# Moving the transposes and stores of aggregates into a later gather: a two-layer graph network on one NeuronCore

## The chip, the cores and the metric

The kernel runs on one core of a Trainium2 chip. The metric is device time in microseconds, from one launch. Of the kernel before there are three runs, and one further execution was recorded by the hardware profiler. A core has five engines that run side by side, each working through its own queue of instructions in the order in which it was laid down: TensorE (PE in the profile; its weight loads are PEld), VectorE (DVE), ScalarE (ACT), GpSimd (POOL) and SyncE (SP, which issues DMAs here). They wait for each other through semaphores.

## What is computed

There are 16 graphs of 1024 nodes with 64 channels, an adjacency matrix for each, and a node mask. The first layer takes, for every node and channel, weighted quantiles over the values of the node's neighbours that are left after some edges have been removed by rank. A small two-layer network follows. The second layer is three graph convolutions. Cut to its core:

```python
h = relu(layernorm(x))
neigh = (adj_ > 0) & ~eye                 # neighbours, without the node itself
rank = cumsum(neigh) - neigh              # a neighbour's number in its row
skip = max(where(nb > 10, (nb + 1) // 2, 1), 1)
rem = neigh & (skip > 1) & (rank % skip == skip - 1) & mask
nd = where(rem | rem.T, 0, adj_) > 0      # live neighbours and the node itself
s = sort(where(nd[..., None], h[:, None], inf), axis=2)
for tau, w in ((0.25, 0.25), (0.5, 0.5), (0.75, 0.25)):
    pos = tau * (nv - 1)                  # nv: live entries of the node
    agg += w * (s[floor(pos)] + frac(pos) * (s[ceil(pos)] - s[floor(pos)]))
x = x + (relu((h + agg) @ W1 + b1) @ W2 + b2) * mask
h = relu(layernorm(x))
x1 = bn(relu(adj @ (h @ W1) + b1)); x2, x3 in the same way from x1, x2
out = x + relu(concat(x1, x2, x3) @ Wl + bl)
```

## The kernel before

**Pairs and blocks.** The graphs are worked on in eight pairs. The 64 channels of the two graphs of a pair fill the 128 partitions. The nodes of a graph are put in the order of their number of live neighbours, `place` holding each node's place. The 1024 places are cut into seven blocks (`BLOCKS`: 0 to 200, 200 to 392, 392 to 592, 592 to 768, 768 to 888, 888 to 960, 960 to 1008) and a tail of 16 (`TAIL`, 1008 to 1024). A block has a fixed number of slots for each node's neighbours, from 11 in the first to 42 in the tail, so that a sort of fixed shape fits all of its nodes.

**Preparing a pair (`prepare`, lines 651 to 842).** Layer norm, the edges and their transpose, the removal of edges (lines 722 to 742, with the result `edge` by ScalarE on line 744 and the sort key on line 750), the rows in their new order through DRAM, and a number for every live neighbour, `r`. This is written as a generator. It is run eleven steps at a time, between the blocks of the pair before, so that both are in flight together.

**A block (`gather_block`, `sort_block`).** `gather` (line 936) goes through the slots in chunks of `per`, about 400 columns together. For each slot VectorE compares `r` with the slot's number, which gives a one-hot tile `s` (line 962; there are two buffers). TensorE multiplies it with the node features, in three bf16 parts, into `pg` (line 993; three buffers in PSUM). ScalarE copies `pg` into the block's `g` (line 998; two buffers of whole blocks). A sort on VectorE follows, a fixed list of minima and maxima over slots (line 920), then the quantiles' coefficients (line 925) and their sum (line 933) into `agg`, one tile of 128 x 1024 per pair.

**Storing.** As soon as 128 further columns of `agg` are complete, `store` (line 1000) has TensorE transpose them (line 1005, into `pt_agg`, one buffer), ScalarE copy the result into `o` (line 1007, two buffers), and ScalarE issue one DMA for each graph of the pair (line 1009) into `agg_d` in DRAM. A pair gives eight such transposes: block 0 gives one, block 1 two, block 2 one, block 3 two, block 4 none, blocks 5 and 6 one each. Pairs 0 to 6 do not sort their tails at once. They lay them down in `tail_d`, and `sort_tails` sorts those of pairs 0 to 3 during pair 4 and those of pairs 4 to 6 during pair 7, with a transpose for each pair; pair 7 sorts its own. That makes 72 transposes in all.

**The order of the work.** The loop of lines 1367 to 1384 has one step per block n: eleven steps of the next pair's preparation, the gather of block n + 1, then the sort of block n, at the end of which its stores are issued. The last pair runs with `later` instead (lines 1389 to 1406), the second half of the network for all pairs, seven steps per block, and what is left of it at the end. `later` reads `agg_d` by an indirect DMA (line 1172). `done.sent` tells how many pairs have been stored completely when the program is built, and an assertion in `first` compares with it. The order in the program is a priority, not yet the order of a queue: a planner lays down each engine's queue ahead of the run, with durations of its own, always taking the ready instruction that stands first in the program. On the chip each queue is then followed as it stands.

The functions that the change touches:

Of the kernel before, what the change touches and what calls it, by code (L numbers as in the profile page):

```python
# [41 lines left out]
TAIL = (1008, 1024, 21, 42)  # L42
# [317 lines left out]
def missing_high(slots, least):  # L360

    return range(slots - 1, least, -2)
# [37 lines left out]
def graph_layers_kernel(ctx: ExitStack, tc: tile.TileContext, ins, out: bass.AP):  # L400
    nc = tc.nc
# [5 lines left out]
    NP = NB // 2  # L407
# [6 lines left out]
    ident = const.tile([P, P], F32, name="ident")  # L414
# [129 lines left out]
    def bias(value):  # L544

        if value not in biases:
            t = const.tile([P, 1], F32, name=f"bias{len(biases)}")
            nc.vector.memset(t, value)
            biases[value] = t
        return biases[value]  # L550
# [22 lines left out]
    TW = TAIL[1] - TAIL[0]  # L573
# [362 lines left out]
    def gather(st, block, g, pools):  # L936


        work, ps, _ = pools
        j0, j1, least, slots = block  # L940
        first, end, fewer = NEAR[(BLOCKS + (TAIL,)).index(block)]
        W = j1 - j0
        high = missing_high(slots, least)
        r, at = (st.r[0], j0) if j1 <= SPLIT else (st.r[1], j0 - SPLIT)
        per = max(1, min(HALF // W, 400 // W))
        for k0 in range(0, slots, per):
            n = min(per, slots - k0)

            w0 = fewer.get(k0, 0)
            if w0 == W:  # L950
                w0 = 0
            chunks = [
                range(
                    max([c for c in first if k0 + k >= first[c]], default=0),
                    min([c for c in end if k0 + k < end[c]], default=NT),
                )
                for k in range(n)
            ]
            s = work.tile([P, n, 2, NT, W], BF16, tag="s", bufs=2, name="s")
            for k, us in enumerate(chunks):  # L960
                us = slice(us.start, us.stop)
                nc.vector.tensor_scalar(  # L962
                    s[:, k, :, us, w0:], r[:, :, us, at + w0 : at + W], float(LIVE + 1 + k0 + k), None, ALU.is_equal
                )
            pg = ps.tile([P, n, W], F32, tag="pg", bufs=3, name="pg")
            looks = [(u, [k for k in range(n) if u in chunks[k]]) for u in range(NT)]
            looks = sorted((look for look in looks if look[1]), key=lambda look: -len(look[1]))
            whole = len(looks[0][1]) == n and not w0
            if not whole:
                for x in range(2):  # L970

                    nc.tensor.matmul(
                        out=pg[x * C : (x + 1) * C].rearrange("p k w -> p (k w)"), lhsT=ident_h[C:, :C],
                        rhs=st.hp[C:].rearrange("p a x t c -> p (a x t c)")[:, : n * W], start=True, stop=False,
                    )
            for i, (u, ks) in enumerate(looks):
                if i == whole:
                    for k in range(n):
                        if k0 + k + 1 not in high:
                            continue  # L980
                        none = work.tile([P, W], BF16, tag="none", bufs=2, name="none")
                        nc.scalar.activation(
                            none, st.nvs[:, j0:j1], AF.Relu, bias=bias(k0 + k + 0.5), scale=-1.0
                        )
                        for x in range(2):
                            half = slice(x * C, (x + 1) * C)
                            nc.tensor.matmul(
                                out=pg[half, k], lhsT=ident_big[:, half], rhs=none, start=False, stop=False
                            )
                ks = slice(ks[0], ks[-1] + 1)  # L990
                for part in range(3):
                    for x in range(2):
                        nc.tensor.matmul(  # L993
                            out=pg[x * C : (x + 1) * C, ks, w0:], lhsT=st.hp[:, part, x, u, :],
                            rhs=s[:, ks, x, u, w0:], start=(whole and i == 0 and part == 0),
                            stop=(i == len(looks) - 1 and part == 2),
                        )
            nc.scalar.copy(g[:, k0 : k0 + n, :], pg)  # L998

    def store(p, agg, cols, place0, pools):  # L1000

        work, ps, _ = pools
        n = cols.stop - cols.start
        pt = ps.tile([P, P], F32, tag="small", bufs=1, name="pt_agg")
        nc.tensor.transpose(pt[:n, :], agg[:, cols], ident)
        o = work.tile([P, P], F32, tag="o", bufs=2, name="o")
        nc.scalar.copy(o[:n, :], pt[:n, :])
        for x in range(2):
            nc.scalar.dma_start(out=agg_d[2 * p + x][place0 : place0 + n, :], in_=o[:n, x * C : (x + 1) * C])

    def gather_block(st, n, pools):
        work, ps, rows = pools
        block = (BLOCKS + (TAIL,))[n]
        j0, j1, _, slots = block
        if n == 0:
            for q in range(len(TAUS)):
                nc.gpsimd.tensor_copy(tail_z[:, q, st.p, :], st.z[:, q, TAIL[0] : TAIL[1]])
        st.g[n] = rows.tile([P, slots, j1 - j0], F32, tag="g", bufs=2, name="g")
        gather(st, block, st.g[n], pools)

    def sort_block(st, n, pools):

        work, ps, rows = pools
        if n == len(BLOCKS) and st.p < NP - 1:
            nc.scalar.dma_start(out=tail_d[st.p][:, :, :], in_=st.g[n])
            return
        block = (BLOCKS + (TAIL,))[n]
        j0, j1, _, slots = block
        if n == 0:
            st.agg = work.tile([P, N], F32, tag="agg", bufs=1, name="agg")  # L1030
            st.done = 0
        t = rows.tile([P, plan(block)[3], j1 - j0], F32, tag="t", bufs=1, name="t")
        quantiles(work, block, (st.g[n], t), st.z[:, :, j0:j1], st.agg[:, j0:j1])
        while st.done + P <= j1 or (j1 >= TAIL[0] and st.done < j1):
            cols = slice(st.done, min(st.done + P, j1))
            store(st.p, st.agg, cols, st.done, pools)
            st.done = cols.stop

    def sort_tails(first, end, pools):

        work, ps, rows = pools
        W = (end - first) * TW
        g = rows.tile([P, TAIL[3], W], F32, tag="g", bufs=2, name="g_tails")
        for p in range(first, end):
            nc.scalar.dma_start(out=g[:, :, (p - first) * TW : (p - first + 1) * TW], in_=tail_d[p][:, :, :])
        t = rows.tile([P, plan(TAIL)[3], W], F32, tag="t", bufs=1, name="t_tails")
        agg = work.tile([P, W], F32, tag="agg_tails", name="agg_tails")
        quantiles(work, TAIL, (g, t), tail_z[:, :, first:end].rearrange("p q p2 w -> p q (p2 w)"), agg)
        for p in range(first, end):
            store(p, agg, slice((p - first) * TW, (p - first + 1) * TW), TAIL[0], pools)  # L1050


    def channels_first(pools, src, tag):
# [295 lines left out]
    with ExitStack() as stack:  # L1349
        keep = stack.enter_context(tc.tile_pool(name="keep", bufs=1))  # L1350
        pools = (
            stack.enter_context(tc.tile_pool(name="work", bufs=1)),
            stack.enter_context(tc.tile_pool(name="ps", bufs=1, space=PSUM)),
            stack.enter_context(tc.tile_pool(name="rows", bufs=1)),
        )
        last = len(BLOCKS)
        with ExitStack() as inner:
# [7 lines left out]
            st = ahead.result  # L1365
            gather_block(st, 0, pools)
            for p in range(NP - 1):
# [16 lines left out]
                st = ahead.result  # L1384


        with ExitStack() as inner:
            one = inner.enter_context(tc.tile_pool(name="late", bufs=1))
            late = (one, inner.enter_context(tc.tile_pool(name="ps_late", bufs=2, space=PSUM)))
            done = Pair()  # L1390
            done.sent = TAILS[NP - 1][0]
            ahead = Steps(later(late, done))
            for n in range(last + 1):
                for _ in range(STEPS):
                    ahead.step()
                if n == 0:
                    sort_block(st, n, pools)
                    gather_block(st, n + 1, pools)
                    sort_tails(*TAILS[NP - 1], pools)
                    done.sent = NP - 1  # L1400
                    continue
                if n < last:
                    gather_block(st, n + 1, pools)
                sort_block(st, n, pools)
            done.sent = NP
            ahead.rest()

# [45 lines left out]
```

## Time and profile before

| | us |
|---|---|
| three runs: median (lowest, highest) | 3244.12 (3240.37, 3251.95) |
| the profiled execution's own time | 3232.01 |
| its span, first instruction to last | 3230.2 |
| TensorE busy, with 27819 matmuls | 2602.9 (81%) |
| VectorE busy | 2569.1 (80%) |
| ScalarE busy | 1714.2 (53%) |
| one transpose on line 1005 (median of the 65 from `agg`) | 0.328 |
| one copy on line 1007 (median of 72) | 0.266 |
| one DMA issue on line 1009 (median of 144) | 0.345 |
| the first transpose of aggregates, the last | 279.9, 2913.8 |

The profile has one row for each group of instructions: the line in the kernel, the engine, the operation, the tile written and those read, and how many. A timeline row gives the start and the length in microseconds, and in brackets how long the engine had been idle before it and what ended that. A row of the list of waits gives who waited for whom, the total in microseconds, how often, and the longest. The mean granted TensorE clock was 0.902 of full speed.

### The profile page before, as it was taken

The numbers are of one execution on the slowest core, as the hardware profiler recorded it, in microseconds if no ns is written. First come the engines' busy times: TensorE is split into PE (matmuls) and PEld (weight loads), VectorE is DVE, ScalarE is ACT, GpSimd is POOL, SyncE is SP. The second block draws the span as 40 slices with busy tenths as digits, with TensorE's granted clock in tenths as the row PEclk, the third lists the DMA queues.
The fourth block names the chain that finished last, engine by engine and source line by source line (L and its number), as shares of the span: only waits on it lengthen the run. The fifth ranks groups of instructions, "written<-read, shape, count | busy, mean of one in ns | idle before, by whom it ended". The sixth has DMA issues, their size and how long they took to land. (4 is left out here: it accounts for less than half of the span.)

```text
span 3230.2 us, 67236 instructions
## 1 busy us (share of the span) xinstructions
PE 2602.9 (81%) x27819; PEld 1728.7 (54%) x27849; DVE 2569.1 (80%) x5895; ACT 1714.2 (53%) x3292; POOL 461.8 (14%) x545
## 2 busy tenths in 40 slices
PE   3689968987898689867686799689976689898878
PEld 2446645664566357545463466456644356565545
DVE  4149999899889988998997889988996888793332
ACT  4777647655766566666464666476553223242221
POOL 4111020110011001200112010201112120221110
PEclk9779989998999799988797799889988799899999
DMA  4131113011311130114001211130102110222211
GB/s 136 46 105 66 37 44 123 33 35 32 118 33 37 42 107 33 51 54 97 31 17 45 91 48 34 45 117 32 39 21 61 21 42 17 54 55 53 53 53 41
DMA packets 221082, 177.45 MB, mean 55 GB/s; under 512 B 189024, under 2 KB 189152, under 8 KB 216672
## 3 DMA queue, kind: packets, MB, share of 16 engines
q1 hardware_dynamic: 141824, 125.88, 12.7%
q0 software_dynamic: 17408, 37.81, 3.8%
q10 hardware_dynamic: 61536, 9.39, 1.9%
q8 instruction: 219, 3.59, 0.5%
q14 instruction: 95, 0.78, 0.1%
HBM read 124.44 MB, written 48.55 MB: 54 GB/s over the span
## 5 line engine op out<-in xcount | busy, mean ns | idle before, releaser
L993 PE MATMUL pg<-s,hp 128*64 128x400 bf16 (+11 forms) x16848 | 1361.8, 314 | 93.2 <-DVE s L962 92.7
L993 PEld LDWEIGHTS <-hp 128*64 128x64 bf16 x16848 | 907.4, 113 | 452.1 <-issue 75.3
L962 DVE TENSOR_SCALAR s<-r 128x3200 bf16<-128x3200 bf16 (+25 forms) x1312 | 621.1, 520 | 144.2 <-PE pg L993 143.9
L998 ACT COPY g<-pg 128x400 f32<-128x400 f32 (+10 forms) x384 | 168.5, 442 | 478.2 <-PE pg L993 440.4
L920 DVE TENSOR_TENSOR t<-g 128x600 f32<-128x600 f32 (+9 forms) x524 | 319.8, 628 | 12.9 <-ACT g L998 11.1
L770 POOL DMA_INDIRECT live_d<-edge,place x128 | 175.4, 1371 | 1025.3 <-DVE place L765 870.9
L1129 PE MATMUL pg<-adjT,xw 128*64 128x512 fp8e4 x2304 | 285.5, 400 | 39.6 <-DVE xw L1119 28.9
L920 DVE TENSOR_TENSOR g<-t 128x96 f32<-128x96 f32 (+16 forms) x555 | 285.8, 539 | 1.4
L855 ACT ACTIVATE coef<-z,bias 128x200 f32<-128x200 f32 (+6 forms) x480 | 174.8, 402 | 140.9 <-DVE agg L933 133.7
L1129 PEld LDWEIGHTS <-xw 128*64 128x64 bf16 x2304 | 144.7, 115 | 163.1 <-DVE xw L1119 30.3
L1172 POOL DMA_INDIRECT agg<-agg_d,place x128 | 139.4, 1089 | 535.7 <-PE pt L1060 412.8
L920 DVE TENSOR_TENSOR t<-t 128x192 f32<-128x192 f32 (+20 forms) x447 | 208.5, 478 | 0.4
L796 PE MATMUL pt<-ident_h,lp 128*128 128x128 bf16 x1024 | 102.3, 261 | 120.8 <-DMA lp<-live_d 71.1
L786 POOL DMA_DIRECT2D lp<-live_d x128 | 87.5, 685 | 774.0 <-PE pt L796 745.4
L664 DVE SCALAR_TENSOR_TENSOR junk_v<-a 128x1024 fp8e4<-128x1024 f32 x128 | 156.3, 1221 | 49.2 <-DMA a<-in_adj 49.0
L858 ACT ACTIVATE coef<-coef,wcol 128x200 f32<-128x200 f32 (+7 forms) x512 | 190.7, 399 | 3.5 <-issue 2.2
L799 ACT ACTIVATE liveT<-pt 128x1024 fp8e4<-128x1024 f32 x128 | 129.9, 1024 | 98.7 <-PE pt L796 97.6
L838 ACT CAST r<-pr 128x592 bf16<-128x592 f32 (+1 forms) x256 | 143.5, 587 | 48.6 <-PE pr L834 47.4
L832 PE MATMUL pr<-liveT,upto 128*128 128x512 fp8e4 (+2 forms) x384 | 124.7, 343 | 50.3 <-ACT r L838 41.3
L796 PEld LDWEIGHTS <-lp 128*128 128x128 fp8e4 x1024 | 82.9, 117 | 145.0 <-DMA lp<-live_d 101.0
L762 ACT ACTIVATE junk<-keys,minus 128x1024 fp8e4<-128x1024 f32 x128 | 144.4, 1128 | 29.8 <-PE keys L755 28.7
L744 ACT ACTIVATE edge<-q,bias 128x1024 fp8e4<-128x1024 f32 x128 | 142.0, 1110 | 33.1 <-PE q L739 29.1
(182 smaller groups left out, 3956.6 us busy)
## 6 DMA issues: line engine op xcount, KB each, us to landing
a<-in_adj SPq DMA_DIRECT2D x128, 512.0 KB, 3.4
adjT_d<-edgeT SPq DMA_DIRECT2D x16, 1024.0 KB, 4.4
lp<-live_d POOLq DMA_DIRECT2D x128, 128.0 KB, 2.3
adjT<-adjT_d SPq DMA_DIRECT2D x16, 1024.0 KB, 6.3
room<-in_x SPq DMA_DIRECT2D x16, 256.0 KB, 3.2
h_d<-room SPq DMA_DIRECT2D x16, 256.0 KB, 2.9
h_again<-h_d SPq DMA_DIRECT2D x16, 256.0 KB, 3.8
xt<-in_x SPq DMA_DIRECT2D x16, 256.0 KB, 4.7
```

The costliest lines, as they stand in the source:

```text
L664: nc.vector.scalar_tensor_tensor(junk, a, 1.0, a, ALU.is_equal, ALU.not_equal, accum_out=odd[:, b, t : t + 1], saturate=False)
L762: nc.scalar.activation(junk, keys, AF.Sign, bias=minus[:, t : t + 1], accum_out=above[:, t : t + 1], saturate=False)
L770: sent = nc.gpsimd.indirect_dma_start(out=live_d[b][:, :], out_offset=bass.IndirectOffsetOnAxis(ap=place[:, b, t : t + 1], axis=0), in_=ed ...
L796: nc.tensor.matmul(out=pt[:, u, :], lhsT=lp[:, u * P : (u + 1) * P], rhs=ident_h, start=True, stop=True)
L838: nc.scalar.copy(st.r[side][:, x, u, :], pr[:, : j1 - j0])
L855: nc.scalar.activation(coef[:, i, :], z[:, at], AF.Abs, bias=bias(rank - (slots + 1) // 2 + tau), scale=sign)
L858: nc.scalar.activation(coef[:, i, :], coef[:, i, :], AF.Relu, bias=wcol[:, q : q + 1], scale=-w)
L920: nc.vector.tensor_tensor(view(bufs, o, n1, n2), view(bufs, a, n1, n2), view(bufs, b, n1, n2), ALU.max if op else ALU.min)
L962: nc.vector.tensor_scalar(s[:, k, :, us, w0:], r[:, :, us, at + w0 : at + W], float(LIVE + 1 + k0 + k), None, ALU.is_equal)
L993: nc.tensor.matmul(out=pg[x * C : (x + 1) * C, ks, w0:], lhsT=st.hp[:, part, x, u, :], rhs=s[:, ks, x, u, w0:], start=(whole and i == 0 an ...
L998: nc.scalar.copy(g[:, k0 : k0 + n, :], pg)
L1129: nc.tensor.matmul(out=pg[cs, :], lhsT=part[:, u, cs], rhs=adjT[x][:, u, sl], start=(u == 0 and k == 0), stop=(u == NT - 1 and k == len(xw ...
```

## The change

`gather` now remembers the last matmul of its last chunk that starts at or before half of the slots, and returns it. Where `sort_block` and `sort_tails` called `store`, they now put the call's arguments on a list, `waiting`. `gather_block` calls `send` after it has traced its gather: `send` runs `store` for all that waits, and every transpose gets an edge to the remembered matmul. That edge carries no semaphore. It only tells the planner that the transpose comes later in TensorE's queue than that matmul. Since block n is sorted after the gather of block n + 1, its stores come with the gather of block n + 2. They move past all of that gather in the program's order, and so do their copies on ScalarE and the DMA issues on ScalarE's queue. Block 6's go with the first gather of the next pair. In pairs 4 and 7, where block 0 is sorted ahead of the gather of block 1, block 0's go with the gather of block 1, and those of `sort_tails` with the gather of block 2. At the end of the last pair a last `send`, without the edge, stores block 6 and the tail.

```diff
-                        nc.tensor.matmul(
+                        summed = nc.tensor.matmul(
                             out=pg[x * C : (x + 1) * C, ks, w0:], lhsT=st.hp[:, part, x, u, :],
...
             nc.scalar.copy(g[:, k0 : k0 + n, :], pg)
-
-    def store(p, agg, cols, place0, pools):
+            if k0 <= slots // 2:
+                halfway = summed
+        return halfway
+
+    waiting = []
+
+    def send(pools, after=None):
+        for one in waiting:
+            store(*one, pools, after)
+        waiting.clear()
+
+    def store(p, agg, cols, place0, pools, after=None):
...
-        nc.tensor.transpose(pt[:n, :], agg[:, cols], ident)
+        turned = nc.tensor.transpose(pt[:n, :], agg[:, cols], ident)
+        if after is not None:
+            tc.add_manual_dep(
+                turned.ins, after.ins.name,
+                mybir.DependencyInfo(mybir.DependencyClass.NoSync, mybir.DependencyReason.SCHED_ONLY),
+                reason="the aggregates are late",
+            )
...
-        gather(st, block, st.g[n], pools)
+        send(pools, gather(st, block, st.g[n], pools))
...
-            store(st.p, st.agg, cols, st.done, pools)
+            waiting.append((st.p, st.agg, cols, st.done))
...
-            store(p, agg, slice((p - first) * TW, (p - first + 1) * TW), TAIL[0], pools)
+            waiting.append((p, agg, slice((p - first) * TW, (p - first + 1) * TW), TAIL[0]))
...
                     sort_tails(*TAILS[NP - 1], pools)
-                    done.sent = NP - 1
                     continue
                 if n < last:
                     gather_block(st, n + 1, pools)
                 sort_block(st, n, pools)
+                done.sent = NP - 1
+            send(pools)
             done.sent = NP
             ahead.rest()
```

## The prediction

> **What bounds the kernel now.** I first read the busy times: TensorE is busy 2602.9 us (81%), VectorE 2569.1 us (80%), ScalarE 53%. No engine is full, so the two busiest must be waiting for each other. The chain of waits reaches back only to 3088 us, 142 us before the end, a stretch that belongs to the second layer, so it says nothing of the change. The list of waits, longest first in total, does:
>
> ```profile
> PE pt_agg L1005 <- DVE agg L933: 96.3, 23, 11.3
> PE pg L993 <- DVE s L962: 92.7, 40, 12.2
> DVE s L962 <- PE pg L993: 143.9, 69, 21.3
> ```
>
> The first line is what the change aims at: 23 times TensorE stood at the transpose of a block's aggregates until VectorE had written them, 96.3 us together, 3.0% of the span. The second and third say that TensorE otherwise waits for the one-hot tiles `s`, and VectorE for TensorE to free them. A microsecond taken from the first line is a gain only where the second does not take it over and VectorE is itself waiting.
>
> Then I listed the 72 transposes with the idle time ahead of each. Seven of them, one per pair (at 481, 788, 1096, 1407, 1785, 2099 and 2404 us), hold 5 x 10.29 + 11.33 + 9.72 = 72.5 us of the 96.3. TensorE's timeline at the third, then VectorE's:
>
> ```profile
> 1084.85 0.53 PE L993 MATMUL pg<-s,hp 128*64 128x32 bf16 x24
> 1095.66 0.47 PE L1005 MATMUL pt_agg<-ident,agg 128*128 128x128 f32 x1 [10.29 <-DVE agg L933]
> 1097.80 1.21 PE L993 MATMUL pg<-s,hp 128*64 128x400 bf16 x6 [1.67 <-DVE s L962]
> ...
> 1089.55 0.19 DVE L962 TENSOR_SCALAR s<-r 128x160 bf16<-128x160 bf16 x1
> ...
> 1095.38 0.23 DVE L933 TENSOR_TENSOR agg<-coef 128x72 f32<-128x72 f32 x1
> 1095.52 3.84 DVE L962 TENSOR_SCALAR s<-r 128x224 bf16<-128x224 bf16 x34
> ```
>
> Here TensorE has finished block 6's gather (1085.4). Next are the transpose of block 5's aggregates and the gather of the last 16 nodes, whose first chunk needs 25 one-hot instructions. VectorE slips these singly between the sort steps of block 5, and most come after `agg`. TensorE stops again at 1097.80 for that very tile. VectorE is without a gap from 1076 to 1106.
>
> The other 16 waits hold 96.3 - 72.5 = 23.8 us. The largest group, five of 1.85 to 2.35 us, lies where a pair's first block is finished beside the matmuls that remove the next pair's edges (lines 728 to 742). At 1204.98 TensorE waits 2.34 us, and VectorE later goes idle for TensorE:
>
> ```profile
> 1204.98 0.33 PE L1005 MATMUL pt_agg<-ident,agg 128*128 128x128 f32 x1 [2.34 <-DVE agg L933]
> ...
> 1220.78 0.17 DVE L750 SCALAR_TENSOR_TENSOR key<-nv,node 128x8 f32<-128x8 f32 x1 [1.34 <-ACT edge L744]
> 1237.84 1.91 DVE L962 TENSOR_SCALAR s<-r 128x3200 bf16<-128x3200 bf16 x2 [0.70 <-PE pg L993]
> 1241.90 1.58 DVE L962 TENSOR_SCALAR s<-r 128x2800 bf16<-128x2800 bf16 x2 [2.15 <-PE pg L993]
> 1245.96 0.64 DVE L962 TENSOR_SCALAR s<-r 128x1824 bf16<-128x1824 bf16 x1 [2.48 <-PE pg L993]
> ```
>
> From 1221 to 1251 TensorE is the bound, so a lead it brings into this stretch reaches the next sort.
>
> **What the Trainium skill says.** "TensorE: Matmul & The Clock Gate", section on the array and engine queue depths: TensorE may pull weight loads ahead, but its matmuls keep program order; ScalarE and VectorE are strict first in, first out. The trace agrees: no gather matmul passes the transpose in the 10.29 us, and VectorE's one-hots keep their place behind the sort. The same page, section on PE-mode transpose: the result lands in PSUM and has to be copied out. Here that copy is 0.27 us on ScalarE (72 of them). "Perfetto Trace Analysis", section on identifying the most-contended engine: matmul busy share is a poor measure of headroom. That agrees with a TensorE at 81% that gates VectorE in one stretch and waits for it in the next.
>
> **The change, part by part.**
>
> 1. The seven tail waits. Removed: 10.29 us and the transpose itself. In its place TensorE goes straight to line 993, which cannot start before its tile is written, at 1097.80. VectorE's queue there has no gap to move into, so the wait of 1.67 us becomes one of 10.29 + 0.47 + 1.67 = 12.4 us. Gain 0, for all seven (each is followed within 2.14 us by a wait of 1.66 or 1.67 us for `s`). If the one-hots did come earlier, 72.5 us would be free; nothing in the edit touches VectorE's code, so I take 0.
>
> 2. The waits of 1.85 to 3.28 us. I followed each to the next idle time of VectorE that TensorE or its follower ended; the lead is worth the smaller of the two. At 586 and 896 us TensorE next waits 0.5 us for `key` on a VectorE that has no gap: 0. At 1205, 1894 and 2205 us VectorE waited for that removal's result 1.34, 1.11 and 1.28 us: 3.73. At 1658 us: 0.21. At 2338 us VectorE then waits 0.76 and 1.23 us for TensorE: 1.99. At 2623 us the lead runs into VectorE's wait of 10.41 us for a gather DMA: 0. Sum 5.9 us. The small ones (0.2 to 0.84 us, 3.4 us together): I take 1. Together 7 us; bounds 0 and 23.8.
>
> 3. ScalarE and the stores. Per block 0.27 us of copy and two DMA issues (median 0.345 us each) move along, 72 and 144 of them. They now stand between the copies of `g` in mid-gather. With ScalarE 53% busy and three `pg` buffers they are hidden; without that cover they would cost 72 x 0.96 = 69 us. One place can gain: where pair 4 sorts the tails, the stores' issue is held up behind the tails' loads.
>
> ```profile
> 1507.36 8.31 ACTq L1009 DMA_DIRECT2D agg_d<-o  x2
> 1515.72 0.48 ACT L998 COPY g<-pg 128x384 f32<-128x384 f32 x1 [11.50 <-issue]
> ```
>
> Block 0's store now comes lower in priority than the whole gather of block 1, so the copies of `g` may pass it, up to 8.3 us. But TensorE then waits 5.10 and 11.75 us for VectorE (1541.87, 1572.69), and VectorE itself waits for the tails' loads until 1517.81. I take 0, bound 8.
>
> 4. The transposes' new place. 72 x 0.33 us = 24 us of TensorE time exists before and after. Before, the two of block 1 stand at the end of the TensorE-bound stretch (1250.75, 1251.43); now they stand in block 3's gather, where VectorE is sorting. Block 0's goes into that stretch from just ahead of it. I count 0, between -5 (two of 0.33 us in eight pairs) and +10. Where two follow each other, the second needs the one `pt_agg` buffer emptied: at most 0.35 us x 16 pairs of transposes = 6 us, hidden if other matmuls stand between, as now. By the middle of that gather the aggregates are ready: the gather fills a `g` buffer which the same sort has to release first. So the new order adds no wait of its own.
>
> 5. Buffers and the end. `agg` is freed by block 6's transpose, which moves into the next pair's first gather; it stands at 1136.66 now, and `agg` is next written by that pair's first sort, which ends at 1204.92, 68 us later. The last pair's stores (2879.72, 2913.81) go after the last sort; the gather DMAs that read them run at 3090. Both hidden. `done.sent` gates only what the builder may issue.
>
> 6. The static order. The order on every engine is laid down before the run from a planner's times. Moving 72 transposes shifts those times by fractions of a microsecond, and may swap one-hots and sort steps on VectorE. The trace can't show the new order; it bounds the size. Between successive tail transposes equal work of one pair takes 307.1, 307.3, 310.9, 313.3 and 305.3 us (the interval with tails left out), so orders and clocks of this kind differ by up to 4 us from their middle. Over 8 pairs that is -24 to +32 us. I take 0.
>
> Sum: -7 us. The profiled execution took 3232.0 us (span 3230.2, 1.8 around it) and would take 3225. It lies 12.1 us below the median of the runs, 3244.1, so by that measure the forecast is **3237 us**.
>
> **The rivals.** What a measurement of this kernel can tell from no change is about 0.3%, 9.7 us: 3234.4 to 3253.9.
>
> - A, the likeliest: the waits are absorbed as worked out, and the order hardly moves. 3237, own range 3229 to 3250. For it: the 1.67 us behind every 10.29.
> - B, faster: the leads of part 2 pass whole (23.8 us), or the new order suits the pairs by 3 us each. 3244 - 24 = 3220. For it: 143.9 us in which VectorE waits for TensorE. Against: two of eight pairs show the lead absorbed at `key`.
> - C, slower: the planner's VectorE list shifts. In each pair, where a sort ends inside the TensorE-bound gather, a chunk's two one-hots (1.9 us) fall behind one combining step (L925, 1.6 us), and TensorE waits 3.5 us. 8 x 3.5 = 28, less the 7: 3265. It decides from (7 + 9.7) / 8 = 2.1 us per pair. For it: the waits come back at the same spot of every pair, so one bad swap counts eight times. Against: the one-hots' code and priorities are unchanged.
> - D: the tail waits go too, because the one-hots move ahead of the sort: 3244 - 96 = 3148. Against it: the sort of block 5 is issued ahead of that gather in the program.
>
> **How the numbers follow.** A 0.50 (0.13 of it below 3234.4, 0.33 within, 0.04 above), B 0.22, C 0.26, D 0.02. Faster 0.13 + 0.22 + 0.02 = 0.37, same 0.33, slower 0.04 + 0.26 = 0.30. The range 3212 to 3270 holds A, the middle of B and C, and part 6's bounds in most of their length; about 0.1 is left out on each side. The likeliest case's own range is 3229 to 3250.
>
> **What would show it.** Right: the line of waits for `agg` at L1005 is all but gone (under 5 us); the wait of `pg` for `s` grows by some 70 us, with 12 us waits once per pair at the tail gather; VectorE's busy time is within 1%. Part 2: no 2 us wait in the removal's matmuls, `key` 1.3 us earlier in its pair. Wrong: VectorE's order differs between the two kernels by more than single instructions, the pairs' period leaves 305 to 313 us, ScalarE waits at the stores' issue in mid-gather, or the tail waits shrink.

## The result, and the profile after

The changed kernel took 3235.66 us in the median of 20 runs, the kernel before 3244.82 us in 20 runs beside it: ratio 0.9968, 95% interval 0.9956 to 0.9980, 9.2 us less between the medians. Measured twice more with the experiments it came to 0.9930 (0.9906 to 0.9955) and 0.9929 (0.9907 to 0.9950). So it is faster, by some 9 to 23 us. The forecast was 3237 us, by a gain of 7 us. On this occasion the number was met; on the later two the gain was about three times the forecast. The experiments show that the reason given for it was not what made the kernel faster.

The profiled execution of the changed kernel has a span of 3234.3 us. That is above the 3230.2 us of before's profile, which happened to be a short execution, so the two spans say nothing of the gain; the single stretches do. First the list of waits (who waited for whom, total us, how often, longest):

```profile
PE pg L993 <- DVE s L962: 150.6, 31, 15.0
...
DVE s L962 <- PE pg L993: 111.1, 62, 9.1
...
PE pt_agg L1017 <- ACT o L1025: 16.2, 7, 2.6
```

The 96.3 us in which TensorE waited for `agg` at the transposes are gone. In their place its wait for `s` grew by 58 us (92.7 before), and there is a new line: transposes that wait for a copy by ScalarE, 16.2 us, nearly nothing before. VectorE's waits for TensorE fell by 33 us (143.9 before; a second profile of before has 128.2, so not all of that is the change). The timeline at the third tail's gather, the place the prediction began with:

```profile
1097.30 0.53 PE L993 MATMUL pg<-s,hp 128*64 128x32 bf16 x24
...
1107.57 0.23 DVE L933 TENSOR_TENSOR agg<-coef 128x72 f32<-128x72 f32 x1
1107.72 3.85 DVE L962 TENSOR_SCALAR s<-r 128x224 bf16<-128x224 bf16 x34
...
1110.00 1.21 PE L993 MATMUL pg<-s,hp 128*64 128x400 bf16 x6 [12.17 <-DVE s L962]
```

The transpose no longer stands ahead of the tail's gather, and TensorE waits 12.17 us for the one-hots instead. The prediction had said 12.4.

Where, then, did time go? The end of each block's `agg` on VectorE cuts the span into stretches. Of the six stretches from one pair's block 6 to the next, five are 302 to 312 us in both profiles and differ by 0 to 4 us. Pair 4's is 381.2 us before and 359.7 after. In its middle the timeline of the kernel before has this (`live_d` are the scatters by which POOL writes the rows of the next pair's second graph in their new order, `lp` the loads that read them back):

```profile
1684.62 4.10 POOL L770 DMA_INDIRECT live_d<-edge,place  x1 [8.30 <-DVE place L765]
...
1689.02 14.40 POOL L770 DMA_INDIRECT live_d<-edge,place  x1 [0.30 <-issue]
...
1703.73 1.22 POOL L770 DMA_INDIRECT live_d<-edge,place  x1 [0.30 <-issue]
...
1711.01 0.96 POOL L770 DMA_INDIRECT live_d<-edge,place  x1 [0.30 <-issue]
...
1714.41 1.89 PE L796 MATMUL pt<-ident_h,lp 128*128 128x128 bf16 x16 [22.35 <-DMA lp<-live_d]
...
1728.65 1.53 DVE L962 TENSOR_SCALAR s<-r 128x1152 bf16<-128x1152 bf16 x4 [21.31 <-PE pg L993]
```

and the changed kernel, at the same place:

```profile
1689.52 4.54 POOL L770 DMA_INDIRECT live_d<-edge,place  x1 [8.12 <-DVE place L765]
...
1694.37 1.96 POOL L770 DMA_INDIRECT live_d<-edge,place  x1 [0.30 <-issue]
...
1696.63 1.26 POOL L770 DMA_INDIRECT live_d<-edge,place  x1 [0.30 <-issue]
...
1705.00 1.18 POOL L770 DMA_INDIRECT live_d<-edge,place  x1 [0.30 <-issue]
...
1708.63 1.98 PE L796 MATMUL pt<-ident_h,lp 128*128 128x128 bf16 x16 [11.88 <-DMA lp<-live_d]
...
1721.51 1.86 DVE L962 TENSOR_SCALAR s<-r 128x1152 bf16<-128x1152 bf16 x5 [9.10 <-PE pg L993]
```

Before, the second of eight scatters took 14.40 us, where the six behind it take 0.96 to 1.5 (the first takes 4.1 to 4.5 in both kernels). The eight lasted 27.3 us (1684.62 to 1711.97), after the change 16.7 us. TensorE waits for the loads that follow, 22.35 us against 11.88, and VectorE for TensorE, 21.31 us against 9.10. The diff touches none of these lines.

It does touch the planner: of VectorE's 5768 instructions in the program's main part 2070 stand at another place in the queue than before, of ScalarE's 3010 others than the stores 1189, of TensorE's 27106 others 8734, of SyncE's 293 45, of POOL's none. So two things changed at once, the place of the stores and the order of everything else.

### The profile page after: what moved, and what is told of

It is laid out like the page before. It is cut to its first block, busy times and chain, and to the rows that moved or that the text cites. A ratio compares the mean times of both kernels' runs of the same rounds, so it can differ in the third digit from the quotient of the medians.

```text
span 3234.3 us, 67196 instructions
## 1 busy us (share of the span) xinstructions
PE 2614.8 (81%) x27819; PEld 1721.7 (53%) x27849; DVE 2568.1 (79%) x5895; ACT 1710.7 (53%) x3292; POOL 468.4 (14%) x545
## 5 line engine op out<-in xcount | busy, mean ns | idle before, releaser
L993 PE MATMUL pg<-s,hp 128*64 128x400 bf16 (+11 forms) x16848 | 1379.6, 314 | 183.0 <-DVE s L962 150.6
L770 POOL DMA_INDIRECT live_d<-edge,place x128 | 159.1, 1243 | 983.9 <-DVE place L765 835.8
L796 PE MATMUL pt<-ident_h,lp 128*128 128x128 bf16 x1024 | 108.9, 274 | 91.9 <-DMA lp<-live_d 45.3
L662 ACT ACTIVATE edge<-a 128x1024 fp8e4<-128x1024 f32 x128 | 133.8, 1055 | 44.2 <-DMA a<-in_adj 43.7
```

Source lines behind the costliest of these rows:

```text
L770: sent = nc.gpsimd.indirect_dma_start(out=live_d[b][:, :], out_offset=bass.IndirectOffsetOnAxis(ap=place[:, b, t : t + 1], axis=0), in_=ed ...
L993: summed = nc.tensor.matmul(out=pg[x * C : (x + 1) * C, ks, w0:], lhsT=st.hp[:, part, x, u, :], rhs=s[:, ks, x, u, w0:], start=(whole and ...
```

## The experiments

**Order or stores.** Both can be held. The program is traced twice: once to learn the planner's queues, and once with an edge from every instruction to the next in each queue, the stores' own instructions left free. An edge of this kind carries no semaphore.

```diff
     with tile.TileContext(nc) as tc:
         graph_layers_kernel(tc, ins, out, late, stores)
+        for engine, order in like.items():
+            mine = by[engine]          # traced, stores left out
+            for a, b in zip(order, order[1:]):
+                tc.add_manual_dep(mine[b], mine[a].name, NO_SYNC, reason="the order of the other kernel")
```

One kernel stores late and holds the order of before, the other stores at once and holds the order of the changed kernel.

> The stores are moved as in the change, and the queues of all five engines are held, instruction for instruction, in the order they have in the kernel before, the stores (transposes, copies, DMA issues) alone standing elsewhere. Direct theory (the prediction's sum): the leads of the waits of 2 us pass in part, the tail waits turn into waits for s: 7 us less, ratio 0.998. Order theory (the planner's new order of everything else brings the gain): no difference, ratio 1.000 within 0.001. Tail theory (the seven waits are a gain that the new order eats up again): 60 to 72 us less, ratio 0.98. In every case the waits for agg at the transposes come to less than 5 us in the profile, and under the direct and the order theory TensorE waits about 12 us for s at each tail's gather.

> The counterpart: the stores are issued at once as in the kernel before, and all else is held in the order that the planner gave the changed kernel. Direct theory: no gain without the late stores, ratio 1.000 within 0.001 against before. Order theory: the whole gain is here, ratio 0.997, and pair 4 is some 20 us shorter than in the profile of before. Tail theory: the new order by itself costs some 60 us, ratio 1.02. The waits for agg at the transposes should stand at 70 to 100 us again.

> The changed kernel once more, beside the two with held orders: ratio 0.995 to 0.998 by all theories. If direct and order effects add, its gain is the sum of the gains of the two held kernels. Its second profile shows which of the differences in pair 4 (11.9 us at the transposes of lp, no hold-up of the copies of g behind a store's issue) come again.

> The kernel before once more, for a second profile. If the 14.4 us scatter of live_d in pair 4 belongs to the order, it comes again, with a wait of 22 us of TensorE for lp at about 1714 us and the hold-up of 11.5 us of the copies of g at 1516 us; if it is an accident of that one execution, the wait is 12 us as in the changed kernel, and the order theory loses some 10 of its 20 us in pair 4.

| | stores | order of the rest | ratio (95%) | pair 4's stretch, us | second or third scatter |
|---|---|---|---|---|---|
| before, again | at once | before's | 1 | 377.0 | 14.40 |
| p1 | late | before's | 1.0012 (0.9993 to 1.0031) | 375.4 | 14.40 |
| p2 | at once | changed | 0.9921 (0.9896 to 0.9945) | 365.3 | 1.96 |
| changed, again | late | changed | 0.9930 (0.9906 to 0.9955) | 359.6 | 1.97 |

The late stores by themselves bring nothing: p1's interval leaves room for some 2 us at most, not for the forecast 7. The planner's order brings the gain, also where the stores stay where they were. The held scatter is no accident of one execution: it took 14.39 to 14.40 us in all five profiles that have before's queues unchanged. (In the two profiles of before the stretch is 381.2 and 377.0 us, so a single one is good to some 4 us.)

**What the late stores do by themselves.** With before's order held, the timeline of p1 shows the tail waits of the prediction (12.45 us at 1106.92) and this:

```profile
371.83 0.33 PE L1017 MATMUL pt_agg<-ident,agg 128*128 128x128 f32 x1
...
372.33 0.33 PE L737 MATMUL q<-edge,ident_h 128*128 128x256 fp8e4 x2
...
373.05 0.43 ACT L998 COPY g<-pg 128x352 f32<-128x352 f32 x1
...
374.91 0.26 ACT L1026 COPY o<-pt_agg 128x128 f32<-128x128 f32 x1
...
375.22 0.48 PE L1017 MATMUL pt_agg<-ident,agg 128*128 128x128 f32 x1 [2.57 <-ACT o L1026]
...
386.18 0.17 DVE L750 SCALAR_TENSOR_TENSOR key<-nv,node 128x8 f32<-128x8 f32 x1 [1.62 <-ACT edge L744]
```

Where a block gives two transposes, the second needs the one `pt_agg` buffer. Its copy stands in ScalarE's queue behind a row of coefficient steps and comes 2.75 us after the transpose (374.91). Only a few matmuls of the edges' removal stand between the two, so TensorE stops for 2.57 us in the middle of the removal. The sort key behind it then waits 1.62 us. This comes six times in p1, each with 2.57 us. With the stores at once these waits of TensorE for the copy come to 0.4 us in all. What the keys lose is less clear. They wait for `edge` 7.5 us in all, against 3.9 and 5.2 us in the two profiles of before (two waits of 11 us in the first pair's own preparation are the same in all and left out here), but two more kernels below with the stores at once and, but for a few instructions, the order of before, s1 and s4, have 7.0 and 8.6 us. So the sum of the keys' waits doesn't tell late stores from early ones. Two kernels measured the parts, both with before's order held; one has no transposes at all:

```diff
+        if late == "left out":
+            for x in range(2):
+                nc.scalar.dma_start(out=agg_d[2 * p + x][place0 : place0 + n, :], in_=ident[:n, x * C : (x + 1) * C])
+            return
         pt = ps.tile([P, P], F32, tag="small", bufs=1, name="pt_agg")
```

> The order of before held on every queue; the 72 transposes of aggregates and their 72 copies are left out, and each store sends a constant tile instead, so that the aggregates do not reach the second layer; the DMAs' number and sizes stay. Direct theory, step 1 (the tail waits are free, since TensorE then waits for s): ratio between 0.997 and 1.001, and TensorE waits about 12 us for s once per pair. Tail theory: 72 to 96 us less, ratio 0.970 to 0.978. Were only the 24 us of the transposes themselves worth their time, ratio 0.993.

Ratio 0.9967 (0.9953 to 0.9981). TensorE waits 12.43 us for `s` at the tails, as expected, and no key waits for `edge` after the first pair's. So even taking out all 72 transposes and their copies is worth 11 us (5 to 15 by the interval), not the 96 us of the list of waits nor quite the 24 us that they last. A better place for them could hardly gain more than that with this order. (The DMA issues stayed in, and the 14.40 us scatter is there too.)

```diff
-            if late:
+            if late and n == 0:
                 waiting.append((st.p, st.agg, cols, st.done))
```

> The order of before held on every queue; only the stores of block 0 of each pair are moved, as in the change. These are the transposes with the waits of 1.85 to 2.35 us ahead of the removal's matmuls, part 2 of the prediction. Direct theory: 3.7 to 6 us less, ratio 0.998 to 0.999; the sort key (line 750) loses its wait of 1.1 to 1.3 us for edge in three pairs. Rival, all leads are absorbed: ratio 1.000. With 5 rounds a difference of this size may stay inside the interval; then the waits of VectorE at the key decide.

Ratio 0.9999 (0.9981 to 1.0017): no gain seen, though 4 us would lie inside the interval. The waits at the keys speak for the rival, though weakly: three of 1.3 to 1.4 us remain, at other pairs (1001, 1995 and 2305 us) than in the first profile of before, and their sum, 4.2 us, lies between those of the two profiles of before, whose waits also stand at different pairs.

**What holds the scatter.** In the profiles with before's order the held scatter ended 0.96 us after the start of one particular instruction of VectorE, the division of the layer norm's 128 x 16 sums (line 559; 1700.45 us in the second profile of before, and the scatter ended at 1701.41). In the changed kernel it stands 13 us earlier. (It is already the layer norm of pair 6, the next pair but one.) This one instruction was moved, each way, with everything else held:

```diff
     order = orders[vector]
+    order.remove(mean[6])
+    order.insert(order.index(summed[6]) + 3, mean[6])   # s2: back, to where the other order has it
```

> The kernel before, stores at once, every queue held in its order, and one instruction moved: in pair 4 the layer norm's division of 128 x 16 sums on VectorE (line 559, 0.17 us, started at 1700.45 in the second profile of before) goes 12.8 us forward, to where it stands in the changed kernel, two instructions behind its reduction. Scatter theory (the second scatter of live_d on POOL is held until VectorE runs that instruction: 14.40 us, and it ends 0.96 us after the start of it): the scatter takes 1 to 3 us, TensorE's wait for lp falls from 22 to about 10 us, pair 4 from 376 to about 366 us, ratio 0.997. Rival, chance of timing (POOL is held by something else): 14.4 us stay, ratio 1.000. If the whole gain of the new order is this one place, ratio 0.993.

> The counterpart: the changed kernel, stores late, its own order held, and the same instruction of pair 4 moved back to where the kernel before has it, 13 us later, behind the aggregates' last sum. Scatter theory: the second scatter takes 12 to 14.4 us again, TensorE waits about 21 us for lp, some 10 us slower than the changed kernel, ratio 0.996 to 0.997 against before where the changed kernel had 0.993. If it is the whole gain: ratio 1.000. Rival: no difference from the changed kernel, 0.993.

The theory of this instruction falls, in both directions: 0.9992 (0.9976 to 1.0008) for the first and 0.9971 (0.9957 to 0.9985) for the second, with pair 4 at 376.7 and 359.5 us. In s2 none of these scatters hangs. In s1 the second scatter did get through at line 559, and the third was held instead (POOL's own timeline, then VectorE's at the end of the hold):

```profile
1689.32 4.10 POOL L770 DMA_INDIRECT live_d<-edge,place  x1 [8.30 <-DVE place L765]
1693.72 1.97 POOL L770 DMA_INDIRECT live_d<-edge,place  x1 [0.30 <-issue]
1696.00 12.15 POOL L770 DMA_INDIRECT live_d<-edge,place  x1 [0.30 <-issue]
...
1706.92 0.39 DVE L920 TENSOR_TENSOR t<-g 128x240 f32<-128x240 f32 x1
1707.35 0.41 DVE L920 TENSOR_TENSOR g<-g 128x240 f32<-128x240 f32 x1
```

No small instruction stands at the end of this hold. But line 559 has been taken from between these two, and there VectorE has nothing under way for 0.03 us, the only such moment in the 12.15 us; elsewhere an instruction starts before the record of the last one ends. The scatter ends 0.8 us after that moment (1708.15). In s2 the place from which line 559 was taken has such a pause too, 0.03 us at 1702.91, and the second scatter ended 0.86 us after it. So one such instruction, or a pause, lets one scatter through. The next kernels give one to each scatter, and, for the price of a delay, hold POOL in the changed kernel:

```diff
         nc.vector.tensor_reduce(stat, xt, AX.X, ALU.add)
+        for _ in range(8):             # in pair 6's layer norm alone; placed one to every three instructions of the held queue
+            nc.vector.tensor_scalar(var, stat, 1.0 / C, None, ALU.mult)
```

> The kernel before, stores at once, its order held, and eight more products of 128 x 16 on VectorE (0.11 us apart each, 1 us in sum, written over afterwards) spread through the 14 us in which the scatter of pair 5's second graph hangs, one to every three instructions. In three kernels a held scatter got through at such an instruction. Theory of the small instruction: each lets one scatter through, the eight scatters end about 10 us sooner, TensorE's wait for lp falls from 22 to 11 to 13 us, and by the scatter theory the ratio is 0.997. Rival (what lets a scatter through is not the instruction): at least one scatter hangs for 10 us or more again, ratio 1.000.

> The changed kernel with its own order held, and 24 writes of 16 elements on POOL (some 0.28 us each with their issue 0.4 to 0.5 us, so 7 to 12 us) between the first and the second scatter of live_d of pair 5's second graph, the place at which the kernel before has its scatter of 14.40 us. Scatter theory (the scatters of that graph set the end of pair 4's middle, whatever holds them): TensorE's wait for lp grows from 12 by as much as the scatters end later, pair 4 and the whole get longer by the same 7 to 12 us: ratio higher than that of the changed kernel in the same call by 0.002 to 0.004. Rival (the delay is taken up later, since VectorE and TensorE lend each other time): no difference between the two.

> The changed kernel a third time, as the measure for the two beside it: ratio 0.993 to 0.997, pair 4 360 us.

The timeline of s4, the scatters and VectorE's added instructions (line 1478) in turn:

```profile
1695.48 1.97 POOL L770 DMA_INDIRECT live_d<-edge,place  x1 [0.30 <-issue]
...
1696.49 0.17 DVE L1478 TENSOR_SCALAR ln_var<-ln_stat 128x16 f32<-128x16 f32 x1
...
1699.29 1.26 POOL L770 DMA_INDIRECT live_d<-edge,place  x1 [0.30 <-issue]
1699.63 0.16 DVE L1478 TENSOR_SCALAR ln_var<-ln_stat 128x16 f32<-128x16 f32 x1
...
1700.86 1.14 POOL L770 DMA_INDIRECT live_d<-edge,place  x1 [0.31 <-issue]
1701.09 0.16 DVE L1478 TENSOR_SCALAR ln_var<-ln_stat 128x16 f32<-128x16 f32 x1
...
1708.66 2.00 PE L796 MATMUL pt<-ident_h,lp 128*128 128x128 bf16 x16 [10.14 <-DMA lp<-live_d]
...
1721.25 1.86 DVE L962 TENSOR_SCALAR s<-r 128x1152 bf16<-128x1152 bf16 x5 [6.75 <-PE pg L993]
```

Six of the eight scatters last until 0.9 to 1.0 us after a small instruction starts (1695.48 + 1.97 = 1697.45 = 1696.49 + 0.96; 1700.86 + 1.14 = 1702.00 = 1701.09 + 0.91); the first ends so behind the reduction of line 558, the last behind a one-hot. And 0.96 us is the shortest that any scatter takes. None hangs. The eight take 15.0 us instead of 27.3, TensorE's wait for `lp` is 10.14 us, pair 4 takes 364.2 us, and the ratio is 0.9971 (0.9956 to 0.9985). One microsecond of further work on VectorE made before's kernel some 9 us faster (0.29% of 3248 us; 5 to 14 by the interval), with its stores and the order of the rest untouched.

In d1 the added writes took less than expected, 4.0 us or 0.17 us each and not 0.28 or more, and the eight scatters ended 2.8 us later after the first than in the changed kernel. TensorE's wait for `lp` is 14.66 us, 2.8 to 3.0 us above the 11.68 to 11.88 of the changed kernel's three profiles, and pair 4 takes 362.5 us against 356.9 to 359.7. The ratio is 0.9940 (0.9926 to 0.9954) beside 0.9929 (0.9907 to 0.9950): the step fits, though by the times alone the two cannot be told apart. s4 and d1 together show, within the 4 us or so to which a single profile is good, that these scatters set the time of pair 4: 12.3 us less of them took 13 to 17 us off it, 2.8 us more added 3 to 6.

**Without the edge.** The last kernel waits with the stores as the change does, but leaves TensorE's place for them to the planner.

```diff
-        if after is not None:
+        if False:
             tc.add_manual_dep(turned.ins, after.ins.name, ...
```

> The change without its edge to the middle of the gather: the stores wait on the list and are issued after the gather, but TensorE's place for them is the planner's choice. Order theory: the planner's new order comes from taking the stores out of their old place, not from the edge; VectorE's order is nearly that of the changed kernel, so the scatters of pair 5's second graph do not hang, pair 4 takes 360 to 366 us, ratio 0.993 to 0.997. Rival: the edge is what matters, ratio 1.000.

The timeline of this kernel at the same scatters:

```profile
1695.84 3.85 POOL L770 DMA_INDIRECT live_d<-edge,place  x1 [7.95 <-DVE t L920]
...
1699.99 1.63 POOL L770 DMA_INDIRECT live_d<-edge,place  x1 [0.30 <-issue]
...
1701.92 13.96 POOL L770 DMA_INDIRECT live_d<-edge,place  x1 [0.31 <-ACT g L998]
...
1714.65 0.40 DVE L920 TENSOR_TENSOR g<-g 128x240 f32<-128x240 f32 x1
1715.15 1.23 DVE L920 TENSOR_TENSOR t<-g 128x480 f32<-128x480 f32 x2
...
1725.02 1.89 PE L796 MATMUL pt<-ident_h,lp 128*128 128x128 bf16 x16 [21.46 <-DMA lp<-live_d]
```

The expectation failed: a scatter hangs again, for 13.96 us, pair 4 takes 372.5 us, and the ratio is 0.9987 (0.9969 to 1.0006). Again the hold ended 0.8 us after VectorE's only pause in it, 0.10 us at 1715.05. Waiting on the list alone doesn't bring the gain. What the edge did by itself isn't isolated here: without it the transposes stood ahead of the tails' gathers again (72.7 us of waits for `agg`), and VectorE's order is about as far from the changed kernel's as from before's (1219 and 1343 of its 5895 instructions stand at another place in the traces). The waits are worth nothing by p1, so the order is the likelier cause.

## Why the prediction was right, and where it was wrong

Over all profiles, the stretch of pair 4 goes with the hang. The seven with a scatter of 12 us or more (before twice, p1, p4, p5, s1, e4) have 372.5 to 381.2 us. The seven without (the changed kernel three times, p2, s2, d1, s4) have 356.9 to 365.3 us. Smaller holds elsewhere don't show in it: five of the six profiles with the changed kernel's order have a scatter of pair 5's first graph held for 6.6 us at about 1590 us, and the shortest stretches all the same. In every other stretch the means of the kernels with before's order and of those with the changed one differ by less than 5 us.

1. **The tail waits are worth 0: right, and shown.** 12.4 us were predicted for the wait that takes their place; it is 12.45 us with the order held and 12.17 us in the changed kernel, and leaving the transposes out does not free it.
2. **The leads of the waits of 2 us bring 7 us: not found.** They went from their places, but the kernel with before's order gained nothing (1.0012), and moving block 0's stores alone gained nothing that could be seen (p5). p4 shows that some time was there, 11 us. The likeliest taker is step 4's new wait; a second `pt_agg` buffer would have tested that, and no run has one.
3. **ScalarE and the stores cost 0: right.** The hold-up of the `g` copies by a store's issue in pair 4 went in the changed kernel, and the stretch that holds it got no shorter (71.6 us to the end of the tails' sum before, 73.8 after). The copies were hidden in ScalarE's time, but not in time for the buffer that they free.
4. **The transposes' new place: this term was too small, and not hidden.** "At most 0.35 us x 16" was taken for the second transpose's wait, from the length of the copy alone. It is 2.57 us six times over, and 16 us in all with a shorter wait or two, since the copy waits behind ScalarE's coefficients; "the new order adds no wait of its own" was wrong. The queue that the buffer's release stands in was not read.
5. **Buffers and the end: nothing in the traces contradicts it.**
6. **The static order: taken as 0, with bounds of -24 and +32 us. Here lies the result.** Its sign could not be seen beforehand, but its place could: the trace of before already had the 22.35 us wait for `lp` and the 14.40 us scatter, and the prediction did not ask what released them. Its estimate was made from the spread of the ordinary pairs' stretches and left pair 4 out.

So the number held by luck: a gain of 7 us that did not come and an order that was counted as nothing exchanged places. Rival B had the order suit "the pairs by 3 us each"; the gain came from one place in one pair. The signs named for a right prediction all came for step 1 (0.4 us of waits for `agg`, 12 us waits at the tails, 58 us more for `s` of the 70 expected, VectorE busy 2568.1 us and 2569.1 before), but they would have come with the order as the cause too. The signs against it were there as well: VectorE's order differed by far more than single instructions, there is a 2.57 us wait among the removal's matmuls, and the keys do not wait less (9.4 us in all after the first pair's, 3.9 to 8.6 with the stores at once and before's order).

What stays open: why the changed order does not hang. From line 559 on, VectorE runs the same 28 instructions in the same order in s1 and in the changed kernel; in the latter the scatters get in between them, in the former not. It is also open how much the order brings besides the hang. The changed kernel was 0.9929 beside s4's 0.9971 on the same occasion, 14 us apart: the intervals overlap, and the mean stretches show no other place. The changed kernel itself was 0.9968 on the first occasion and s2, without a hang, 0.9971 on another, so ratios of different occasions can differ by 0.4% with nothing changed.

## What to carry to other kernels

A wait in the list is worth what is late next: 96 us of waits for `agg` went with a gain of 11 us even where the transposes themselves were left out. Where a planner lays down the queues, moving a few instructions can move thousands. Hold the order of the rest and measure the two apart before an effect is put down to the edit; a gain from a lucky order may go with the next edit. Before moving a producer of a single buffer, read the queue in which the instruction stands that empties it.

## What the hardware showed

A scatter issued by POOL can be held for 14 us by a VectorE that runs without a gap. The Trainium skill, "SBUF — State Buffer", section "SBUF: two separate sides", says that VectorE and GpSimd share a pair of ports under an exclusive lock, taken by VectorE instructions in a two-port mode or, against GpSimd work that reads SBUF, with two inputs, and that GpSimd, which writes the descriptors of its own DMAs, is locked out meanwhile. That gives a possible reason for the holds, but the fit is loose. What let scatters through, a reduction and products of 128 x 16, has one input each. The 28 instructions that started during the hang in before's second profile were 17 two-input steps of sort, coefficients and sums, and 11 bf16 one-hots, which have one input too. Which of all these run in a two-port mode no trace tells. The page has the holder keep the lock for one instruction; here the hang went on over 13.4 us of back-to-back ones, and the same instructions let the scatters in one after another in the changed kernel. That the lock is the cause is inferred, not shown; what the runs show is that small instructions of 0.16 us each, put in between, let the scatters through, and that two other holds ended at a pause of VectorE of 0.03 and 0.10 us.
